# A block's weights and columns ahead of its rows on SyncE's queue, in the routed experts of a graph network

## The chip, the cores and the metric

One core of one Trainium2 chip runs the whole program in one launch. The metric is device time in microseconds (us). Names of the engines: PE is TensorE's matmul (PEld its weight loads), DVE is VectorE, ACT is ScalarE, POOL is GpSimd and SP is SyncE, which does no arithmetic and issues most of the DMAs. Each engine runs its own queue in order, and engines wait for one another and for DMAs by semaphores.

## The reference, cut to what matters

A graph of 3125 nodes with 256 features goes through four pairs of layers, each pair a graph layer and a feed-forward layer with a residual: attention over 53125 edges and a small mixture of experts; a three-layer convolution and a routed mixture of experts; a normalised convolution and a dense mixture of eight experts; a mean convolution and a sliced attention. The change touches the second feed-forward layer alone:

```python
logits = xt @ Wr + br
probs = jax.nn.softmax(logits, axis=-1)
top_p, top_idx = jax.lax.top_k(probs, TOP_K)          # TOP_K = 2 of 8 experts
weights = top_p / top_p.sum(axis=-1, keepdims=True)
xn = (xt - mu) * jax.lax.rsqrt(var + LN_EPS)
xe = xn[None, :, :] * ln_g[:, None, :] + ln_b[:, None, :]
h = jax.nn.gelu(jnp.einsum('end,edh->enh', xe, W1) + b1[:, None, :], approximate=False)
y = jnp.einsum('enh,ehd->end', h, W2) + b2[:, None, :]
y_tok = jnp.transpose(y, (1, 0, 2))
sel = jnp.take_along_axis(y_tok, top_idx[:, :, None], axis=1)
out = (weights[:, :, None] * sel).sum(axis=1)
```

Here D is 256 and the hidden size H is 1024, so an expert's `W1` and `W2` are 1 MB each.

## The kernel before, in words

Where the reference computes every expert for every token, the kernel computes only the two chosen ones. While the last layer of the convolution runs, `Router` takes each group of tokens as it is ready: `normed` normalises it, `gated` makes the gates, `placed` works out each token's place in its expert's list and scatters its row (256 features and 4 numbers: token, two gates, first expert) to `xs_d` in HBM with an indirect DMA of GpSimd (line 997), once for each of its two experts, and `shifted` adds the gated `b2` and stores x to `x_d`. The scatters are collected in `sent`.

`experts1` then pads each expert's list to blocks of 256 rows (BLK) and works out two small tables on VectorE: `block_e`, the expert of each block, and `block_i`, the block's place in `xs_d` (lines 1056 to 1075). SyncE loads these into registers, eight entries at a time (lines 1086 and 1089), because the addresses of its DMAs depend on them. At least 26 blocks (LEAST) run; up to six more would follow behind branches on `block_n`, and in this execution none does.

`block` handles one block:

- its rows `xs` (128 x 2 x 260, 260 KB) come from `xs_d` by a DMA on SyncE's queue (line 1098). `loads_after` makes that DMA wait for all scatters in `sent`. The tile has three buffers;
- its weights and columns come by `Packer.put` (line 181), three DMAs on SyncE's queue into one slot `wslot`: `w1` and `w2`, 1 MB each, and `c`, 13 columns for each partition with the scale and shift of the normalisation, the bias of the first product and the expert's number. The slots rotate through two buffers, so the weights of block i+2 wait until block i has read its own;
- VectorE works out the target rows `to` and the gate from `xs` and `c` (lines 1109 to 1115);
- PE transposes the rows, four 128 x 128 transposes into two PSUM tiles `tr` (line 1120), and VectorE evacuates each with scale and shift into one half of `xe` (line 1122);
- PE makes the hidden layer in eight groups `hid_ps`, each with two products (k = 0 and 1, one for each half of `xe`), into two PSUM buffers; ScalarE empties each with the bias and GELU into `hid` (line 1129). The products are recorded at line 233, in the helper `product`, and each is two records in the profile;
- PE multiplies `hid` by `w2` into `po`, for each of the two halves of the rows; VectorE applies the gate (`ys`, line 1134), and GpSimd adds the rows to `x_d` with an accumulating indirect DMA (line 1135).

The order in the source is not the order on the engines: a scheduler places the instructions on each engine's queue by data that it expects to arrive, while DMAs on SyncE's queue are issued in the order that it gives them. After the last block x is read back from `x_d` and the next convolution starts. `v_rows` (memset at line 2249) is a tile of the later layers that takes over space that the router's tiles had.

Of the kernel before, what the change touches and what calls it, by code (L numbers as in the profile page):

```python
# [22 lines left out]
N, D = 3125, 256  # L23
# [45 lines left out]
def gnn_ffn_kernel(ctx: ExitStack, tc: tile.TileContext, a, out: bass.AP):  # L69
# [157 lines left out]
    def product(ps, terms, bias=None):  # L227

        last = len(terms) - 1
        if bias is not None:  # L230
            nc.tensor.matmul(ps, ones_h[:, :ps.shape[0]], bias, start=True, stop=False)  # L231
        for i, (l, r) in enumerate(terms):
            nc.tensor.matmul(ps, l, r, start=(bias is None and i == 0), stop=(i == last))  # L233
# [110 lines left out]
    def loads_after(loads, sent):  # L344
        for ld in loads:
            for st in sent:
                tc.add_manual_dep(ld.ins, st.ins.name, data_dep, reason="all rows scattered")
# [671 lines left out]
    def experts1(route=None, ahead=lambda: None):  # L1019
# [4 lines left out]
        ec_d = dram.tile([ne, 128, 13], F32, name="ec_d")  # L1024
        with ExitStack() as es:
# [58 lines left out]
            def run(b0, n):  # L1084

                _, at = nc.values_load_multi_w_load_instructions(
                    block_e[0:1, b0:b0 + n], engines=[mybir.EngineType.SP], min_val=0, max_val=ne - 1,
                    skip_runtime_bounds_check_because="a count of 7 comparisons lies in 0..7")
                _, places = nc.values_load_multi_w_load_instructions(
                    block_i[0:1, b0:b0 + n], engines=[mybir.EngineType.SP],  # L1090
                    min_val=0, max_val=8 * EB,
                    skip_runtime_bounds_check_because="a minimum with the last block's place")
                for e, place in zip(at, places):
                    block(e, place)

            def block(e, place):
                xs = pool.tile([128, R, DX], F32, name="xs", bufs=3)
                ld = nc.sync.dma_start(xs, xs_d.rearrange("(b r p) d -> b p r d", p=128, r=R)[
                    ds(place, 1)].rearrange("b p r d -> p (b r) d"))
                loads_after([ld], sent)  # L1100
                wp = Packer()
                w1 = wp.put(a["ex1_W1"][ds(e, 1)].rearrange("e (k p) n -> p (e k) n", p=128), 128,
                            (2, 1024))
                w2 = wp.put(a["ex1_W2"][ds(e, 1)].rearrange("e (k p) n -> p (e k) n", p=128), 128,
                            (8, D))
                c = wp.put(ec_d[ds(e, 1)].rearrange("e p c -> p (e c)"), 128, (13,))
                to = pool.tile([128, R], I32, name="to", bufs=3)
                one, two = (pool.tile([128, R], F32, name=v) for v in ("one", "two"))
                nc.vector.tensor_scalar(one, xs[:, :, R_TOKEN], 0.0, behind, ALU.is_equal, ALU.mult)
                nc.vector.scalar_tensor_tensor(to, xs[:, :, R_TOKEN], -1.0, one, ALU.add, ALU.add)  # L1110
                gate = pool.tile([128, R], F32, name="gate", bufs=3)
                for w, col, op in ((one, R_TOP, ALU.is_equal), (two, R_SECOND, ALU.not_equal)):
                    nc.vector.scalar_tensor_tensor(w, xs[:, :, R_FIRST], c[:, 12:13], xs[:, :, col],
                                                   op, ALU.mult)
                nc.vector.tensor_add(gate, one, two)
                xe = pool.tile([128, 2, BLK], F32, name="xe")
                for k in range(2):
                    ps = psum.tile([128, 512], F32, name="tr")
                    for r in range(R):
                        nc.tensor.transpose(ps[:, r * 128:(r + 1) * 128],  # L1120
                                            xs[:, r, k * 128:(k + 1) * 128], ident)
                    nc.vector.tensor_scalar(xe[:, k, :], ps[:, :BLK], c[:, k:k + 1],  # L1122
                                            c[:, 2 + k:3 + k], ALU.mult, ALU.add)
                hid = pool.tile([128, 8, BLK], F32, name="hid")
                for m in range(8):
                    ps = psum.tile([128, 512], F32, name="hid_ps")
                    product(ps[:, :BLK], [(w1[:, k, m * 128:(m + 1) * 128], xe[:, k, :])
                                          for k in range(2)])
                    nc.scalar.activation(hid[:, m, :], ps[:, :BLK], AF.Gelu, bias=c[:, 4 + m:5 + m])  # L1129
                ys = pool.tile([128, R, D], F32, name="ys")  # L1130
                for r in range(R):
                    po = psum.tile([128, D], F32, name="po")
                    product(po, [(hid[:, m, r * 128:(r + 1) * 128], w2[:, m, :]) for m in range(8)])
                    nc.vector.tensor_scalar(ys[:, r, :], po, gate[:, r:r + 1], None, ALU.mult)
                    nc.gpsimd.indirect_dma_start(
                        out=x_d, in_=ys[:, r, :], in_offset=None, compute_op=ALU.add,
                        out_offset=bass.IndirectOffsetOnAxis(ap=to[:, r:r + 1], axis=0))
# [1185 lines left out]
```

## Time and profile before

| What | Value |
|---|---|
| median of 3 runs | 3920.74 us (3905.55 to 3923.41) |
| the profiled execution | 3903.86 us, its span 3901.7 us |
| PE busy in the span | 3373.3 us (86%) |
| DVE, ACT, POOL busy | 1726.0, 1029.0, 608.9 us |
| mean granted TensorE clock | 0.887 of full speed |
| rows `xs` loaded, first and last issue | 2294.7 and 2647.6 us, 26 times |
| transposes of a block's rows | 104 of 273 ns |
| products `hid_ps` and `po` of the routed blocks | 832 records each, means 387 and 379 ns |
| `hid` on ACT | 208 of 473 ns |

Times within the span are in us from its start. A busy PE is a pipelined one, so its busy time is no measure of how close it is to its peak; what counts for a change is which wait ends last in the stage that it touches. The granted clock is the share of full speed at which TensorE was allowed to run. In a line of the timeline stand the start, the length of the group, the engine, the line of the code, the operation with output and inputs, the number of instructions, and in square brackets the engine's idle time ahead of it with what ended it. In a line of the waits stand the waiting engine and operation, the releaser, and the total, the number and the longest of the waits.

### The profile page before, as it was taken

Reading aid. Unit: us, or ns where it says so; the run is one execution under the profiler, and the core shown is the slowest. Engines: PE = TensorE matmul, PEld = TensorE weight load, DVE = VectorE, ACT = ScalarE, POOL = GpSimd, SP = SyncE. Lnnn points to the kernel's source line nnn. Section 1 sums busy time; section 2 is a strip of 40 time slices with the busy share of each in tenths; the row PEclk is TensorE's granted clock in tenths of the full one; section 3 lists DMA queues with packets and bytes.
Section 4 is the critical chain, followed back from the end, with each engine's and each line's share of the span. In section 5 each row is a group of like instructions: output and inputs, shape, how many; then the busy total and the mean of one; then the engine's idle time right before and its main releaser. Section 6 shows DMA issues by size and latency. Waiting matters only on the chain.

```text
span 3901.7 us, 45135 instructions
## 1 busy us (share of the span) xinstructions
PE 3373.3 (86%) x16645; PEld 2512.7 (64%) x16645; DVE 1726.0 (44%) x4687; ACT 1029.0 (26%) x1931; POOL 608.9 (16%) x588
## 2 busy tenths in 40 slices
PE   6466766766678998999999969997999999999998
PEld 2345545555456566898988858886885555568765
DVE  5345655655676656232335641113562111154562
ACT  1111111111214223333333312222433232242120
POOL 1445445445110000000001222221000000000000
PEclk9677777777768888999999979998989999999998
DMA  5444444444225544434443346665430000023101
GB/s 170 149 143 144 124 138 144 127 134 146 73 66 198 182 162 130 113 99 108 100 105 79 106 126 180 187 170 147 111 86 16 8 17 8 14 69 102 39 1 34
DMA packets 265707, 415.30 MB, mean 106 GB/s; under 512 B 40860, under 2 KB 206273, under 8 KB 265473
## 3 DMA queue, kind: packets, MB, share of 16 engines
q1 hardware_dynamic: 200242, 261.56, 22.9%
q0 software_dynamic: 51568, 134.33, 12.5%
q10 hardware_dynamic: 13663, 16.39, 1.6%
q8 instruction: 135, 2.21, 0.2%
q14 instruction: 99, 0.81, 0.1%
HBM read 313.72 MB, written 98.40 MB: 106 GB/s over the span
## 4 chain that ended last, share of the span: by engine, by line
PE 61%; DVE 2%; DMA 1%; ACT 1%; issue 0%; POOL 0%; SPq 0%; ACTq 0%; DVEq 0%; POOLq 0%
PE po L233 19%; PE agg L2057 18%; PE hid_ps L233 13%; PE tr L233 2%; PE row L233 1%; PE tok L1436 1%; PE po L231 1%; PE tr L223 1%; DMA x_d<-ys,to 1%; PE tr L2131 1%; PE bk L1966 1%; PE bk L1954 0%; ACT h L1277 0%; PE bdeg L1956 0%; PE pair L233 0%
## 5 line engine op out<-in xcount | busy, mean ns | idle before, releaser
L2057 PE MATMUL agg<-cnt_f,hp 125*128 125x500 f32 (+1 forms) x3500 | 734.4, 370 | 24.0 <-ACT hp L1998 24.0
L2057 PEld LDWEIGHTS agg<-cnt_f,hp 125*128 125x128 f32 x3500 | 638.7, 190 | 108.4 <-ACT hp L1998 25.3
L1556 POOL DMA_INDIRECT kv<-kv_d,src_w x450 | 437.4, 972 | 468.5 <-PE acc L1777 323.9
L2035 ACT CAST cnt_f<-blk 125x500 fp32r<-125x500 bf16 (+1 forms) x435 | 245.9, 566 | 479.4 <-PE agg L2057 464.1
L1732 PE MATMUL qx<-q_t,oht 125*128 125x256 bf16 x1350 | 260.2, 357 | 128.8 <-issue 76.8
L2035 DVE CAST cnt_f<-blk 125x500 fp32r<-125x500 bf16 (+1 forms) x440 | 185.2, 422 | 293.3 <-PE agg L2057 249.5
L1732 PEld LDWEIGHTS <-oht 125*128 125x128 bf16 x1350 | 165.5, 125 | 200.6 <-issue 150.5
L1283 DVE SCALAR_TENSOR_TENSOR x<-po,gall,x 125x256 f32<-125x256 f32 x200 | 93.8, 484 | 416.2 <-PE po L233 415.7
L1277 ACT ACTIVATE h<-hid_ps,shift,scale 128x500 f32<-128x500 f32 (+1 forms) x224 | 161.7, 722 | 376.0 <-PE hid_ps L233 375.5
L1777 PE MATMUL acc<-kv,oh_f 128*125 128x265 f32 x900 | 211.6, 395 | 20.3 <-DVE kv L1770 20.3
L1735 DVE TENSOR_TENSOR kv<-kv,qx 128x512 f32<-128x512 f32 x225 | 147.0, 681 | 146.2 <-remote 122.0
L1777 PEld LDWEIGHTS acc<-kv,oh_f 128*125 128x125 f32 x900 | 169.8, 191 | 59.3 <-DVE kv L1770 28.0
L233 PE MATMUL hid_ps<-xe,wslot 128*128 128x256 f32 x832 | 194.8, 387 | 11.3 <-DVE xe L1122 11.2
L233 PE MATMUL po<-wslot,h 128*125 128x256 f32 x800 | 203.0, 386 | 0.1
L233 PE MATMUL hid_ps<-h,wslot 128*128 128x500 f32 (+1 forms) x448 | 192.5, 552 | 4.1 <-ACT h L1277 0.6
L233 PEld LDWEIGHTS po<-wslot,h 128*125 128x125 f32 x800 | 145.0, 187 | 75.2 <-ACT h L1277 27.2
L233 PE MATMUL hid_ps<-v_rows,wslot 128*128 128x500 f32 (+1 forms) x448 | 187.2, 538 | 0.0
L233 PE MATMUL po<-wslot,hid 128*128 128x256 f32 x832 | 183.8, 379 | 0.0
L233 PEld LDWEIGHTS hid_ps<-xe,wslot 128*128 128x128 f32 x832 | 148.8, 191 | 44.7 <-DVE xe L1122 14.4
L997 POOL DMA_INDIRECT xs_d<-r_l,pos x50 | 59.5, 1190 | 723.0 <-DVE r_l L993 598.9
L233 PEld LDWEIGHTS po<-wslot,hid 128*128 128x128 f32 x832 | 158.1, 190 | 21.5
L1129 ACT ACTIVATE hid<-hid_ps,wslot 128x256 f32<-128x256 f32 x208 | 96.8, 473 | 279.9 <-PE hid_ps L233 279.9
(480 smaller groups left out, 4683.2 us busy)
## 6 DMA issues: line engine op xcount, KB each, us to landing
wslot<-in_ex_W SPq DMA_DIRECT2D x52, 1024.0 KB
blk<-an_d SPq DMA_DIRECT2D x60, 546.9 KB
xs_d<-nothing SPq DMA_DIRECT2D x10, 2730.0 KB
blk<-at_d SPq DMA_DIRECT2D x40, 546.9 KB
blk<-an_d SPq DMA_DIRECT2D x45, 410.2 KB
at_d<-ab SPq DMA_DIRECT2D x25, 683.6 KB
an_d<-an SPq DMA_DIRECT2D x25, 683.6 KB
blk<-at_d SPq DMA_DIRECT2D x30, 410.2 KB
```

Of the source, the lines that this page charges most:

```text
L223: nc.tensor.transpose(ps[:, i * P:(i + 1) * P], src[:, i, k * 128:(k + 1) * 128], ident[:P, :P])
L233: nc.tensor.matmul(ps, l, r, start=(bias is None and i == 0), stop=(i == last))
L997: st = nc.gpsimd.indirect_dma_start(out=xs_d, in_=l2[:, i, :], in_offset=None, out_offset=bass.IndirectOffsetOnAxis(ap=self.pos[s][:, t0 + ...
L1129: nc.scalar.activation(hid[:, m, :], ps[:, :BLK], AF.Gelu, bias=c[:, 4 + m:5 + m])
L1277: nc.scalar.activation(dst[:, m, :c], ps[:, :c], AF.Relu, bias=shift[:, l, col:col + 1], scale=scale[:, l, col:col + 1])
L1283: nc.vector.scalar_tensor_tensor(x[:, t0 + i, :], po, gating.all[:, t0 + i, e:e + 1], x[:, t0 + i, :], ALU.mult, ALU.add)
L1556: nc.gpsimd.indirect_dma_start(out=kv[:, c, KO:], out_offset=None, in_=kv_d, in_offset=bass.IndirectOffsetOnAxis(ap=src_i[:, at + c:at + c ...
L1732: nc.tensor.matmul(ps[:, c, :], s.oht[:, p * PC + c0 + c, :], s.q[:, k, :], start=(k == 0), stop=(k == 2))
L1735: nc.vector.tensor_mul(k_, k_, ps)
L1777: nc.tensor.matmul(s.acc[:, :D + H + 1], of[:, c, :], kv[:, c, AO:VO], start=(p == 0 and c == 0), stop=(p == 2 and c == PC - 1))
L2035: to(f[:, :n, :], part[0][:, :n, m % MB, :])
L2057: nc.tensor.matmul(ps[f][:, :c], hp[:, m, k, f * 128:(f + 1) * 128], got[:, :c], start=(m == 0 and k == 0), stop=(m == T - 1 and k == 1))
```

## The change

In `block` the three DMAs of the packer move ahead of the DMA of the rows, and among them the columns `c` move ahead of the two weights. On SyncE's queue a block's DMAs stood as rows, W1, W2, columns; they now stand as columns, W1, W2, rows. Nothing is added or removed, and the dependencies are the same: only the rows wait for the scatters.

```diff
             def block(e, place):
+                wp = Packer()
+                c = wp.put(ec_d[ds(e, 1)].rearrange("e p c -> p (e c)"), 128, (13,))
+                w1 = wp.put(a["ex1_W1"][ds(e, 1)].rearrange("e (k p) n -> p (e k) n", p=128), 128,
+                            (2, 1024))
+
+                w2 = wp.put(a["ex1_W2"][ds(e, 1)].rearrange("e (k p) n -> p (e k) n", p=128), 128,
+                            (8, D))
                 xs = pool.tile([128, R, DX], F32, name="xs", bufs=3)
                 ld = nc.sync.dma_start(xs, xs_d.rearrange("(b r p) d -> b p r d", p=128, r=R)[
                     ds(place, 1)].rearrange("b p r d -> p (b r) d"))
                 loads_after([ld], sent)
-                wp = Packer()
-                w1 = wp.put(a["ex1_W1"][ds(e, 1)].rearrange("e (k p) n -> p (e k) n", p=128), 128,
-                            (2, 1024))
-                w2 = wp.put(a["ex1_W2"][ds(e, 1)].rearrange("e (k p) n -> p (e k) n", p=128), 128,
-                            (8, D))
-                c = wp.put(ec_d[ds(e, 1)].rearrange("e p c -> p (e c)"), 128, (13,))
```

## The prediction

> **What bounds the kernel now.** I read the page first, for the weight of each engine, then the change's stage alone: the timeline and the windows around the routed blocks.
>
> ```profile
> span 3901.7 us, 45135 instructions
> ...
> PE 3373.3 (86%) x16645; PEld 2512.7 (64%) x16645; DVE 1726.0 (44%) x4687; ACT 1029.0 (26%) x1931; POOL 608.9 (16%) x588
> ```
>
> PE is the engine to follow, and the stage is PE's more than the rest: the 26 blocks run from 2294.7 us (first rows issued) to 2689.8 us (last matmul: 2682.77 + 7.07), and from 2322.33 to 2689.80 the windows give PE 363.73 us busy of 367.47, at a granted clock of 1.00. So no transfer holds the steady blocks; only a change in PE's own order or in what PE waits for can move them. The waits of this stretch say the same. Each line is who waited for whom: us in total, times, longest.
>
> ```profile
> DVE one L1113 <- DMA wslot<-ec_d: 189.8, 23, 9.2
> ...
> PE hid_ps L233 <- DVE xe L1122: 3.6, 6, 0.6
> ...
> PEld hid_ps L233 <- ACT hid L1129: 4.9, 24, 0.6
> ```
>
> The first is the largest wait that the change removes: VectorE stands 8.3 us in each block for the columns `c`, which land behind 2 MB of weights. But PE is hardly behind it: it waited 3.6 us for `xe`, in six blocks.
>
> Those six are what the forecast rests on. The order of the built programs shows why. In before, the transposes of the next block are spread through PE's queue among the matmuls of the present one, in a cycle of four blocks. Every fourth block (starting at 2365.50, 2424.28, 2483.07, 2541.85, 2600.63, 2659.42) has all four transposes of its own directly ahead of its first product. PE's timeline of a block without transposes and of the one after it (start, us, group, idle before):
>
> ```profile
> 2351.67 7.09 PE L233 MATMUL hid_ps<-xe,wslot 128*128 128x256 f32 x32
> 2358.59 7.07 PE L233 MATMUL po<-wslot,hid 128*128 128x256 f32 x32
> ...
> 2365.50 0.60 PE L1120 MATMUL tr<-ident,xs 128*128 128x128 f32 x4
> 2366.69 1.99 PE L233 MATMUL hid_ps<-xe,wslot 128*128 128x256 f32 x8 [0.59 <-DVE xe L1122]
> 2368.52 0.38 PE L1120 MATMUL tr<-ident,xs 128*128 128x128 f32 x2
> 2368.87 5.45 PE L233 MATMUL hid_ps<-xe,wslot 128*128 128x256 f32 x24
> 2374.15 7.07 PE L233 MATMUL po<-wslot,hid 128*128 128x256 f32 x32
> 2381.06 0.38 PE L1120 MATMUL tr<-ident,xs 128*128 128x128 f32 x2
> ```
>
> The block without transposes takes 13.83 us (2351.67 to 2365.50), the next one 15.56 (2365.50 to 2381.06), the two others of a cycle 14.70 each: 58.79 for four, 14.70 on average.
>
> **Steady blocks in the changed program.** Its order on PE is the same for every block: four transposes, 16 products into `hid_ps`, 16 into `po`; nothing of the next block lies between. The scheduler now sees rows that arrive after the weights and puts the transposes last. So every block has the shape of the 15.56 us block. Its parts: 1.19 us from the transposes to the first product (0.60 of transposes, 0.59 idle until VectorE has `xe`), and then a second hole. The first four products stand as m0 k0, m1 k0, m0 k1, m1 k1 in both programs' blocks of this shape, so the first GELU starts late (2368.34, 0.47 us long, so done at 2368.81), and the third group, which needs its PSUM buffer, starts at 2368.87. In before, two transposes of the next block fill this hole (0.38 us). In the changed program nothing does, but the start at 2368.87 is set by ScalarE, not by them, so taking them out should give nothing back. Bounds: at best the hole goes with them, and the block takes 13.82 + 1.19 = 15.01; at worst it stays, 15.56. I take 15.56: the weight load of the third group waited 0.20 us for ScalarE even after the two transposes.
>
> The sum: blocks 1 to 25 run from 2322.33 to 2689.84 = 367.51 us. Changed: 24 x 15.56 + 15.72 for the last (2365.50 to the end of its `po`, 2374.15 + 7.07) = 389.16. That is **+21.65 us**. With 15.01 it is about +7.9.
>
> **Do the rows still come in time?** The rows of block i+2 now stand behind the columns and both weights of block i+2, and these wait for the slot that block i's last `po` frees. In before SyncE issues block i+3's rows right after block i+2's columns, a whole block earlier. From the freed slot (first weight issue) to the columns, the last of the 2 MB, it took 9.06 us (2351.83 to 2360.89), in others 8.7 to 10.1 (2498.93 to 2508.99). The rows add 260 KB: at 2.1 MB in 9.1 us, 1.2 us more, so they land 10 to 11.4 us after the slot is free. Their transposes come one block later, 15.56 us. Over 4 us of cover, so I cost the lost block of lead at nothing; if that cover went, each us of lateness would cost 25 us. VectorE now waits for rows instead of columns, ahead of `ys` of the present block; `ys` is ready some 12 us into it, so it is late by a fraction of a us, with two `po` buffers behind it.
>
> **The first block.** The change's promise lies here: weights that need not wait for the rows' scatters. But the block's expert number does not come earlier.
>
> ```profile
> 2287.12 1.19 POOL L997 DMA_INDIRECT xs_d<-r_l,pos  x1 [0.30 <-issue]
> 2291.40 0.18 DVE L1070 TENSOR_TENSOR be<-be,ge 1x32 f32<-1x32 f32 x1 [6.10 <-DMA xs_d<-r_l,pos]
> 2291.42 0.08 DVE L2249 MEMSET v_rows<- 128x25 f32 x1
> ...
> 2292.95 0.16 DVE L1073 CAST block_e<-be 1x32 int32<-1x32 f32 x1
> ...
> 2294.74 0.43 SPq L1098 DMA_DIRECT2D xs<-xs_d  x1
> ```
>
> VectorE stands 6.10 us for the last scatter, because a memset of `v_rows` (into freed space that the scatters still read) is queued among the operations that make `block_e`; it is there in the changed program too. `block_e` is cast 0.31 us before `block_i`, and that is all the weights gain. The same bytes (rows, two weights, columns) then stand ahead of the first product, but the rows are last: in before the last of them let VectorE go at 2305.53, after the four transposes were long done at 2298.8. Now those (1.09 us, at a clock of 0.50), the small VectorE work and the first `xe` (0.54 us) follow the landing: first product 0.4 to 1.0 us later than 2306.39. Block 0 loses the two transposes that it carries for block 1 (0.2 to 0.4). I take **+0.5**, bounds -0.5 and +2 (the clock stays at 0.52 from 2306.39 to 2310.20, and where it rises may shift). Nothing after the stage is overlapped with it: PE's next work waits for x to be read back.
>
> **Clock.** The granted clock was 1.00 in the 15.56 us block in spite of its hole of 0.59 us, so I price the new holes at their length alone. The Trainium skill, "TensorE: Matmul & The Clock Gate", section "A second HAM failure mode: psum-queue depth-cycling", speaks against this: frequent short idles between groups of matmuls can make the clock fall and rise. With that page's window of about 3.4 us at half rate in each of 25 blocks, an estimate is 1.7 x 25 = some 43 us more.
>
> **Total.** 21.65 + 0.5 = +22.15. The profiled execution took 3903.86 (2.2 around its span), so it would become 3926.0. The three runs have their median at 3920.74, 17 us above; on it the forecast is **3942.9**. What a measurement of this kernel can tell from no change is about 0.5%, 19.6 us; the forecast is just beyond it.
>
> **The rivals.**
> 1. The second hole closes without the two transposes: 15.01 per block, +7.9 + 0.5 = +8.4, 3929.1. For it: nothing of the next block is left on PE. Against: ScalarE's time above.
> 2. Rows late: if contention with the weights and with the scatters to `x_d` pushes rows from 11.4 to 16 us after the slot is free, each block waits 0.5 us or more: +12.5 on top, about 3955. The cover of 4 us speaks against it.
> 3. Not slower: the first block's weights do run ahead of the scatters, and the steady blocks keep 14.70. It decides where `block_e` reaches SyncE before the last scatter has landed (2287.12 + 3.84 = 2290.96). VectorE had 2 us of work left after its stand (2291.40 to 2293.43), so `block_e` could be there near 2287, the weights issued 1.3 us later (as 2293.43 to 2294.74) and landed 9.1 us after that, the rows 1.2 us behind them at 2298.6, and the first product some 1.5 us on, near 2300.1, 6.3 us earlier: 3920.74 - 6.3 = 3914.4. Against it: the memset's place, and PE's order, which alone costs over three times that. To be faster by over 0.5% all blocks would have to come near 13.83, with transposes that cost nothing.
>
> **How the numbers follow.** Forecast 0.66, of which 0.14 is taken as falling just under 19.6 us; rival 1 0.12; rival 2 or the clock 0.14; rival 3 0.08, of which 0.05 beyond the bound through what I have not seen. Slower: 0.52 + 0.14 = 0.66. Same: 0.14 + 0.12 + 0.03 = 0.29. Faster 0.05. Range: low end rival 1 on the lowest run, 3905.55 + 8.4 = 3914; high end the forecast with rival 2 on the highest, 3923.41 + 22.15 + 12.5 = 3958. The forecast alone spans 3927.7 to 3945.6 over those runs.
>
> **What would show it.** Right: 25 starts of four transposes 15.5 us apart; PE waiting for `xe` some 0.6 us in each of 25 blocks (15 us instead of 3.6) and its weight loads for ScalarE; VectorE's long wait put down to `xs` instead of `ec_d`; `block_e` still at about 2293. Wrong: PE waiting for `xs` in steady blocks, a period near 15.0 or 14.7, a granted clock under 1.00 there, or a first product well before 2306.

## The result, and the profile after

The changed kernel takes 3941.81 us (median; 3936.1 to 3946.88) against 3920.31 us (3905.55 to 3923.41) before: a ratio of 1.0058, 95% interval 1.0041 to 1.0074, or +21.5 us (+16 to +29). The forecast was +22.15 us and 3942.9 us.

The page of the changed kernel, its first lines:

```profile
span 3945.0 us, 45106 instructions
...
PE 3391.3 (86%) x16645; PEld 2518.3 (64%) x16645; DVE 1730.0 (44%) x4687; ACT 1029.4 (26%) x1931; POOL 609.5 (15%) x588
```

PE runs as many instructions as before and is busy 18 us longer. The two spans differ by 43.3 us, twice what the runs show, so the difference has to be cut up first. The stage is measured here, and in every experiment, from the matmul that adds up the tokens' counts (line 1050, just ahead of `block_e`) to the issue that reads x back after the last block. Ahead of the stage the profiled execution lost 15.87 us (2296.34 against 2280.47), behind it 6.02 (1211.31 against 1205.29), and in it 21.41 (437.35 against 415.94). Only the stage holds changed code, and its 21.41 us agree with the 21.5 by which the medians differ. The rest is taken as the difference between two executions: the runs of before alone lie 18 us apart.

The waits of the steady blocks (2322 to 2712 us; engine and operation, releaser, total us, times, longest):

```profile
DVE one L1110 <- DMA xs<-xs_d: 208.6, 24, 9.9
...
PEld hid_ps L233 <- DVE xe L1123: 19.9, 24, 0.8
PE hid_ps L233 <- DVE xe L1123: 14.2, 24, 0.6
PEld hid_ps L233 <- ACT hid L1130: 14.0, 24, 0.6
PE hid_ps L233 <- ACT hid L1130: 4.2, 23, 0.2
```

VectorE's long wait has changed its name from `ec_d` (189.8 us, longest 9.2) to `xs` (208.6, longest 9.9). PE's wait for `xe` has gone from six blocks to each of the 24 in the window, and a wait that before had once (0.2 us) now comes in nearly every block: the third group of products waits for ScalarE. There is no PE wait for a DMA. PE's timeline of one block:

```profile
2368.47 0.60 PE L1121 MATMUL tr<-ident,xs 128*128 128x128 f32 x4
2369.66 1.99 PE L233 MATMUL hid_ps<-xe,wslot 128*128 128x256 f32 x8 [0.59 <-DVE xe L1123]
2371.83 5.45 PE L233 MATMUL hid_ps<-xe,wslot 128*128 128x256 f32 x24 [0.18 <-ACT hid L1130]
2377.12 7.10 PE L233 MATMUL po<-wslot,hid 128*128 128x256 f32 x32
2384.05 0.60 PE L1121 MATMUL tr<-ident,xs 128*128 128x128 f32 x4
```

It has the shape of the longest of the four blocks in before's cycle, 15.58 us (2368.47 to 2384.05), and every block has it: the transposes of blocks 1 to 25 start from 2337.35 to 2711.37, 24 steps of 15.58 us. The windows give the whole stretch of blocks 1 to 25 at full clock (us, then busy PE, PEld, DVE, ACT, POOL with their instructions, clock, DMA share, GB/s):

```profile
2337.35:2727.12 389.77, 370.45 (x1701) 306.43 (x1699) 66.07 (x220) 92.44 (x200) 77.55 (x50) 1.00 0.57 164
```

389.77 us against 367.51 (2322.33 to 2689.84 in before), so +22.26. The first block went the other way. Its timeline:

```profile
2307.29 0.18 DVE L1070 TENSOR_TENSOR be<-be,ge 1x32 f32<-1x32 f32 x1 [6.12 <-DMA xs_d<-r_l,pos]
...
2308.85 0.16 DVE L1073 CAST block_e<-be 1x32 int32<-1x32 f32 x1
...
2310.07 0.39 SPq L181 DMA_DIRECT2D wslot<-ec_d  x1
2310.67 0.96 SPq L181 DMA_DIRECT2D wslot<-in_ex_W  x2
...
2312.75 0.37 SPq L1105 DMA_DIRECT2D xs<-xs_d  x1
...
2319.56 0.23 DVE L1110 TENSOR_SCALAR one<-xs,behind 128x2 f32<-128x2 f32 x1 [10.23 <-DMA xs<-xs_d]
...
2319.67 1.09 PE L1121 MATMUL tr<-ident,xs 128*128 128x128 f32 x4 [22.75 <-DMA xs<-xs_d]
...
2320.97 7.24 PE L233 MATMUL hid_ps<-xe,wslot 128*128 128x256 f32 x21 [0.21 <-DVE xe L1123]
```

and, for the same place in before, the lines that the prediction did not show:

```profile
2295.98 0.96 SPq L181 DMA_DIRECT2D wslot<-in_ex_W  x2
...
2305.53 0.22 DVE L1113 SCALAR_TENSOR_TENSOR one<-xs,wslot 128x2 f32<-128x2 f32 x1 [7.51 <-DMA wslot<-ec_d]
...
2306.39 3.78 PE L233 MATMUL hid_ps<-xe,wslot 128*128 128x256 f32 x8 [7.60 <-DVE xe L1122]
```

From the end of the stand for the scatters (2307.29, before 2291.40) to the first product it took 13.68 us against 14.99, and to block 1 30.06 against 30.93: -0.87 us (-0.85 from the start of the stage).

### The profile page after: what moved, and what is told of

It is laid out like the page before. It is cut to its first block, busy times and chain, and to the rows that moved or that the text cites. A ratio compares the mean times of both kernels' runs of the same rounds, so it can differ in the third digit from the quotient of the medians.

```text
span 3945.0 us, 45106 instructions
## 1 busy us (share of the span) xinstructions
PE 3391.3 (86%) x16645; PEld 2518.3 (64%) x16645; DVE 1730.0 (44%) x4687; ACT 1029.4 (26%) x1931; POOL 609.5 (15%) x588
## 3 DMA queue, kind: packets, MB, share of 16 engines
q0 software_dynamic: 51568, 134.33, 12.5%
## 4 chain that ended last, share of the span: by engine, by line
PE 61%; DVE 3%; DMA 2%; ACT 1%; issue 1%; POOL 0%; SPq 0%; ACTq 0%; DVEq 0%; POOLq 0%
PE po L233 19%; PE agg L2058 18%; PE hid_ps L233 13%; PE tr L233 2%; PE row L233 1%; PE tok L1437 1%; PE po L231 1%; PE tr L223 1%; DMA x_d<-ys,to 1%; PE tr L2132 1%; PE bk L1967 1%; PE bk L1955 0%; ACT h L1278 0%; PE bdeg L1957 0%; PE s L233 0%
```

## The experiments

The theory on trial is the prediction's: the time goes into PE's order (all four transposes of a block directly ahead of its own products, with two holes behind them), the transfers themselves cost nothing, and the order comes from the place of the rows. Against it stand the rivals that it is the transfers (rows or weights that land late, or compete), or another part of the change. What each expected of a run is quoted with the run.

Four runs (the columns alone, the rows alone, the change with three buffers, the change with the memset moved) share a chip on which before takes 3609.36 us; the other four share one on which it takes 3916.17 us. The 300 us lie ahead of the stage: its first matmul starts at 1978 to 1981 us on the one, at 2284 to 2290 on the other, and at 2280 and 2296 in the two profiles above. So lengths of the stage are compared across both chips, and times only as ratios. A length of the stage comes from one profiled execution of each kernel, and block 0 in it varies by up to 1.4 us with the moment at which the clock rises (last section); the steady blocks do not. Period is the mean distance of steady blocks.

| kernel | ratio of times, 95% interval | stage, us | against 415.94 |
|---|---|---|---|
| the change | 1.0058 (1.0041 to 1.0074) | 437.35 | +21.41 |
| columns ahead of the weights, rows first as before | 1.0000 (0.9991 to 1.0009) | 413.44 | -2.50 |
| rows behind the weights and columns | 1.0056 (1.0041 to 1.0072) | 434.74 | +18.80 |
| the change, three PSUM buffers `hid_ps` | 1.0028 (1.0018 to 1.0039) | 426.02 | +10.08 |
| before, three PSUM buffers `hid_ps` | 1.0029 (1.0017 to 1.0041) | 426.06 | +10.12 |
| the change, memset of `v_rows` on GpSimd | 1.0058 (1.0044 to 1.0071) | 431.81 | +15.87 |
| before, products pipelined in the source | 0.9977 (0.9966 to 0.9987) | 404.92 | -11.02 |
| the change, products pipelined in the source | 1.0035 (1.0020 to 1.0049) | 429.75 | +13.81 |
| the parts that paid, together | 0.9947 (0.9931 to 0.9964) | 399.35 | -16.59 |

### Which half of the change: the columns alone, the rows alone

Columns alone, against before:

```diff
 ld = nc.sync.dma_start(xs, ...)
 loads_after([ld], sent)
 wp = Packer()
+c = wp.put(ec_d[...], 128, (13,))
 w1 = wp.put(a["ex1_W1"][...], 128, (2, 1024))
 w2 = wp.put(a["ex1_W2"][...], 128, (8, D))
-c = wp.put(ec_d[...], 128, (13,))
```

> Only the columns move: rows, columns, W1, W2. Theory A (the cost sits in PE's order, which follows the place of the rows): the cycle of four blocks stays, 58.8 us for four, so no loss in the steady blocks; the first product needs the columns and W1 instead of the columns behind W2, so it starts up to 5 us after W1 instead of after everything: 0 to -6 us against before. Theory B (the columns' place makes the scheduler or VectorE late): blocks of 15.59 us, some +20 us against before.

Measured: no difference in time, 1.0000 (0.9991 to 1.0009). PE's four-block cycle is kept in the build and in the profile: PE waits for `xe` in 7 blocks, not in all. PE's timeline of block 0 and the start of block 1:

```profile
2002.11 9.39 PE L233 MATMUL hid_ps<-xe,wslot 128*128 128x256 f32 x32 [3.32 <-DMA wslot<-in_ex_W]
2011.34 7.10 PE L233 MATMUL po<-wslot,hid 128*128 128x256 f32 x32
2018.28 0.60 PE L1120 MATMUL tr<-ident,xs 128*128 128x128 f32 x4
2019.47 1.99 PE L233 MATMUL hid_ps<-xe,wslot 128*128 128x256 f32 x8 [0.59 <-DVE xe L1122]
```

With the columns early, `xe` is ready before W1, and the first product needs W1 alone, not all 2 MB: it starts 21.55 us after the count's matmul against 25.92. Of these 4.4 us, 1.9 are given back by a longer block 0 and because the cycle now starts with a long block (block 1 stands above, in the 15.56 us shape): the stage is 2.50 us shorter, which the time is too coarse to show.

Rows alone, against before (on SyncE's queue W1, W2, columns, rows):

```diff
-xs = pool.tile([128, R, DX], F32, name="xs", bufs=3)
-ld = nc.sync.dma_start(xs, ...)
-loads_after([ld], sent)
 wp = Packer()
 w1 = wp.put(a["ex1_W1"][...], 128, (2, 1024))
 w2 = wp.put(a["ex1_W2"][...], 128, (8, D))
 c = wp.put(ec_d[...], 128, (13,))
+xs = pool.tile([128, R, DX], F32, name="xs", bufs=3)
+ld = nc.sync.dma_start(xs, ...)
+loads_after([ld], sent)
```

> Only the rows move: W1, W2, columns, rows. Theory A (PE's order follows the place of the rows): the same shape in every block as with the whole change, 15.59 us each, +20 to +23 us against before. Theory B (the columns make it): the cycle of four stays and the time is that of before, within 4 us.

Measured: 1.0056 (1.0041 to 1.0072), about the whole loss of the change (18.80 us in the stage, a little under the 20 expected), with a period of 15.56 us. Its waits in the steady blocks:

```profile
PE hid_ps L233 <- DVE xe L1122: 14.8, 25, 0.6
PEld hid_ps L233 <- ACT hid L1129: 14.0, 24, 0.6
...
PE hid_ps L233 <- ACT hid L1129: 4.2, 23, 0.2
```

They are those of the changed kernel. So the rows' new place is what costs. Of the 2.6 us that the change's stage is longer, 1.9 lie ahead of block 1, 1.3 of them in block 0 itself; blocks 1 to 25 differ by 0.7 us, so in them the columns' new place is worth 0.03 us each.

### Transfers or PE's order: a third PSUM buffer, with each order of the DMAs

If the second hole is the wait for a PSUM buffer that ScalarE has to empty, one buffer more closes it, and the other products and transfers stay as they are. Against the change, and the same line against before:

```diff
-ps = psum.tile([128, 512], F32, name="hid_ps")
+ps = psum.tile([128, 512], F32, name="hid_ps", bufs=3)
```

> The whole change with three PSUM buffers for hid_ps instead of two. Theory A (two holes per block: 0.59 us for xe, and about 0.4 us until the first GELU frees a PSUM buffer): the second hole closes, the first stays; 15.1 to 15.2 us a block, 10 to 12 us less than the changed kernel, +9 to +12 against before; PE's wait for ScalarE goes. Rival (the period is set by the rows' arrival or by the slot): still 15.59 us, +21.

> The DMA order of before (rows first, columns last) with three PSUM buffers for hid_ps; in this build PE's order has the four transposes of each block directly ahead of its own products, as in the change. Theory A (the loss is PE's order; where rows and columns stand on SyncE's queue costs nothing once PE's order is given): the same 15.13 us a block as the change with three buffers, so +9 to +12 us against before. Rival (the DMA order itself costs): rows are a block early here, so blocks of 14.7 us or less and the time of before or better.

Measured: 1.0028 (1.0018 to 1.0039) and 1.0029 (1.0017 to 1.0041). PE's timeline of the change with three buffers:

```profile
2064.50 0.60 PE L1121 MATMUL tr<-ident,xs 128*128 128x128 f32 x4
2065.70 7.17 PE L233 MATMUL hid_ps<-xe,wslot 128*128 128x256 f32 x32 [0.59 <-DVE xe L1123]
2072.71 7.09 PE L233 MATMUL po<-wslot,hid 128*128 128x256 f32 x32
2079.64 0.60 PE L1121 MATMUL tr<-ident,xs 128*128 128x128 f32 x4
```

and of before with three buffers:

```profile
2376.56 0.60 PE L1120 MATMUL tr<-ident,xs 128*128 128x128 f32 x4
2377.75 7.17 PE L233 MATMUL hid_ps<-xe,wslot 128*128 128x256 f32 x32 [0.59 <-DVE xe L1122]
2384.76 7.07 PE L233 MATMUL po<-wslot,hid 128*128 128x256 f32 x32
2391.67 0.60 PE L1120 MATMUL tr<-ident,xs 128*128 128x128 f32 x4
```

The 32 products run through in one line; the hole between the first eight records and the others is gone, and the block takes 15.13 us on average instead of 15.58. PE's only wait left is the one for `xe`, 14.8 us in 25 blocks. From block 1 to the end of the stage before takes 374.08 us, the change 396.34 and the change with three buffers 385.05. So of the change's 21.41 us the second hole is 11.29, the transposes that stand alone ahead of `xe` are 10.97, and the first block is -0.85.

The pair tells more than either run. With three buffers the scheduler gives before the uniform order too, four transposes, 16 products, 16 products. Now both kernels have the same order on PE and differ only in the order of DMAs: in the one the rows come a block early and the columns last, in the other the reverse. Their periods are 15.13 and 15.11 us, and from block 1 on they take 385.05 and 384.61 us; that the whole stages agree to 0.04 us (426.02 and 426.06) is luck, for block 0 differs by as much the other way. So in steady blocks the transfers' order by itself costs at most 0.02 us each, 0.4 in all; what it does, it does through the order that PE's queue is built in. Before, with its DMAs where they were, loses 10.12 us of the stage once it has this order. The pair also shows that late rows are not the only thing that brings the uniform order about: a hole in the scheduler's plan that asks to be filled seems to be needed as well, and the third buffer takes it away. That is read from the built orders; the scheduler's reasons were not tested.

### The stand for the scatters: the memset on another engine

Against the change, the memset that keeps `block_e` behind the last scatter goes to GpSimd:

```diff
-nc.vector.memset(v[:, :, D:], 1.0)
+nc.gpsimd.memset(v[:, :, D:], 1.0)
```

> The whole change with the memset of v_rows on GpSimd, behind its scatters, instead of VectorE, where block_e stands behind it. Theory A (block_e is held by that memset alone): SyncE issues the first weights about 1.3 us after a block_e that comes some 6 us earlier, they land while the scatters run, and the first product starts 4 to 7 us earlier; the steady blocks keep 15.59 us; +14 to +18 against before. Rival (the weights' slot or the transfers hold the first block): no gain, +21.

Measured: 1.0058 (1.0044 to 1.0071); the time alone does not tell it from the change. The profile does:

```profile
1986.77 0.23 DVE L1073 CAST block_e<-be 1x32 int32<-1x32 f32 x1
...
1988.69 0.39 SPq L181 DMA_DIRECT2D wslot<-ec_d  x1
1989.29 0.96 SPq L181 DMA_DIRECT2D wslot<-in_ex_W  x2
1991.19 0.14 POOL L2250 MEMSET v_rows<- 128x25 f32 x1 [3.21 <-DMA xs_d<-r_l,pos]
1991.38 0.37 SPq L1105 DMA_DIRECT2D xs<-xs_d  x1
```

`block_e` stands 6.6 us after the count's matmul (1980.1) instead of 12.5, and columns and weights are issued ahead of the landing of the last scatter, for which only GpSimd's memset and the rows' DMA still wait. The first product comes 4.2 us earlier than in the change (20.43 against 24.63 after the count), and the stage is 5.54 us shorter; from block 1 to the end it is the change's to the hundredth (396.34 us in both). The other 1.34 us are a shorter block 0, in which the clock rose earlier; that is no part of the mechanism. The gain rests on this one profile: by the medians the run is 20.9 us slower than before, not the 14 to 18 expected. This is rival 3's mechanism, with the memset that held it named rightly: against before the first product comes 5.5 us earlier, where the prediction put 6.3.

### What the change would do to another order on PE

In these two kernels the source is pipelined: `block` is split into loads with transposes (`block`), the hidden products (`hidden`) and the output products (`output`), and the next block's rows are transposed between the hidden and the output products of the present one.

```diff
+                for e, place in run(b0, min(8, LEAST - b0)):
+                    following = block(e, place)
+                    if got is not None:
+                        output(got, hid)
+                    got = following
+                    hid = hidden(got)
+            output(got, hid)
...
-                run(b0, min(8, LEAST - b0))
```

> The DMA order of before with the same source order; the built order has the four transposes between the hidden layer and the output. Theory A: no hole is left, only the transposes' own 0.43 to 0.5 us: 13.82 + 0.5 = 14.3 us a block against 14.70, 8 to 11 us less than before. Rival (xe or GELU still shows): 14.7 us, no gain.

> The change's DMA order, with the source written so that a block's loads, transposes and xe stand between the hidden layer and the output of the block before; the built order has the four transposes after six of the sixteen output products. Theory A: both holes go; but the rows are wanted 9.5 us after the slot is free (6.91 + 6 x 0.43) and land 10 to 11 us after it, so PE waits for them 0.5 to 1.4 us in each block: 14.8 to 15.7 us a block, +2 to +24 us against before, put down to xs. Rival (rows are never late): 14.3 us a block, 10 to 12 us less than before.

Measured: with before's order of DMAs 0.9977 (0.9966 to 0.9987), with the change's 1.0035 (1.0020 to 1.0049). PE's timeline of the first:

```profile
2371.37 7.09 PE L233 MATMUL hid_ps<-xe,wslot 128*128 128x256 f32 x32
2378.30 0.60 PE L1124 MATMUL tr<-ident,xs 128*128 128x128 f32 x4
2378.73 7.07 PE L233 MATMUL po<-wslot,hid 128*128 128x256 f32 x32
2385.64 7.09 PE L233 MATMUL hid_ps<-xe,wslot 128*128 128x256 f32 x32
```

PE's waits in the steady blocks are gone, for `xe` and for ScalarE, and the period is 14.27 us, below before's mean of 14.70: the evacuation to `xe` now lies beside 16 output products, and both halves are there before the block begins. The second, with the rows behind the weights (here the scheduler put the transposes after six of the 16 output products):

```profile
2378.96 2.76 PE L233 MATMUL po<-wslot,hid 128*128 128x256 f32 x12
...
2382.32 0.63 PE L1124 MATMUL tr<-ident,xs 128*128 128x128 f32 x4 [0.61 <-DMA xs<-xs_d]
...
2382.79 4.50 PE L233 MATMUL po<-wslot,hid 128*128 128x256 f32 x20
2387.13 7.09 PE L233 MATMUL hid_ps<-xe,wslot 128*128 128x256 f32 x32
```

Its PE has two waits in the steady blocks:

```profile
PE tr L1124 <- DMA xs<-xs_d: 18.2, 23, 1.8
PE tr L1124 <- SPq L1164: 1.8, 1, 1.8
```

Here PE does wait for rows, in each of 24 blocks, 20.0 us in all (18.2 put down to the DMA itself, 1.8 to SyncE), and the steps between blocks are 15.0 to 16.3 us, 15.33 on average. So the order of the DMAs that costs next to nothing when PE takes the transposes last costs 24.83 us (429.75 - 404.92) when it takes them early, 20.0 of them in this wait (the place of the transposes among the output products differs between the two as well): rival 2, late rows, is real in this kernel and absent in the changed one.

### Together

This kernel pipelines the source, keeps rows, columns, W1, W2 for the steady blocks, uses columns, W1, W2, rows for block 0 alone (`first`), and has the memset on GpSimd:

```diff
-            def block(e, place):
+            def block(e, place, first=False):
...
+                if not first:
+                    xs = rows()
 wp = Packer()
 ...
+                if first:
+                    xs = rows()
```

> Pipelined source order; for the first block alone columns, W1, W2, rows; for all others rows, columns, W1, W2; memset of v_rows on GpSimd. Theory A: 14.3 us a block (-9 us) and a first product 4 to 6 us earlier: 13 to 16 us less than before (ratio 0.9957 to 0.9964). Rival (the first block is bound by 2.4 MB of transfers whatever the order): only the 9 us.

Measured: 3896.80 us against 3916.17, 0.9947 (0.9931 to 0.9964), so half a per cent under before, and somewhat more than the 13 to 16 us expected (16.59 in the stage). Its period is 14.29 us, and its first product comes 20.42 us after the count, as in the run with the memset moved.

## Why the prediction was right, and where one term was wrong

**PE's order, right.** Every block took the 15.56 us shape (15.58 measured), 389.16 us predicted for blocks 1 to 25 and 389.77 measured. The first hole is 0.59 us as read from before's long block.

**The second hole, right.** The choice between 15.01 and 15.56 went to ScalarE and the PSUM buffer, and the third buffer shows that this is the wait. Rival 1, a hole that closes with the two transposes, is out. Its 15.01 was a little low: with the hole closed by a buffer the block takes 15.13.

**The rows, right, for a reason that does not carry far.** In the steady blocks they were in use on VectorE 9.9 to 11.2 us after the columns' issue (2369.09 to 2379.18 and 2384.35 to 2394.40 are two), about the 10 to 11.4 predicted and ahead of the 15.58 at which PE asks for them. (The 9.06 us of the prediction starts at 2351.83, which in the chain of work is the start of a row of products; the weights' issue stands at 2351.97, which makes it 8.92 and leaves the cover as it was.) But the cover was there because PE's order had moved the transposes to the end. The pipelined pair shows what the same lateness costs without it, 0.83 us of PE's wait in each block.

**The clock, right.** It was granted at 1.00 from 2337.35 to 2727.12 with two holes in every 15.58 us. The fall that the Trainium skill's page "TensorE: Matmul & The Clock Gate" describes under "A second HAM failure mode: psum-queue depth-cycling", an estimated 43 us, did not occur with these holes of 0.59 and 0.18 us; at what holes it would was not tried.

**The first block, wrong in size and sign.** Predicted +0.5 (bounds -0.5 to +2), measured -0.87. The first product, forecast 0.4 to 1.0 us later, came 1.31 us earlier after the stand (13.68 against 14.99). The term that failed is "`block_e` is cast 0.31 us before `block_i`, and that is all the weights gain". `block_e` itself came no earlier (1.56 us after the stand, before 1.55), as predicted. But the weights' issue came 1.20 us earlier (3.38 us after the stand, before 4.58): in before they stood on SyncE's queue behind the rows' issue, and 1.24 us lie between the two issues (2294.74 to 2295.98), while behind the columns it is 0.60 (2310.07 to 2310.67); the other 0.56 is the first issue itself, 2.78 us after the stand instead of 3.34. From the weights' issue to the last landing that VectorE waits for it took 8.89 us against 9.55 to that point, 0.66 less; why was not tried. The tail behind the last landing grew by 0.55 (1.41 us from VectorE's start to the first product, before 0.86), as the prediction had reasoned. Block 0 itself, where 0.2 to 0.4 less was expected, took 0.44 more (16.38 against 15.94), because the clock rose later. The windows of 1 us in which it rose, before's first and then the change's:

```profile
2309.40:2310.40 1.00, 1.00 (x5) 0.71 (x5) 0.00 (x0) 0.19 (x1) 0.00 (x0) 0.67 1.12 321
...
2325.00:2326.00 1.00, 1.00 (x4) 0.82 (x3) 0.05 (x1) 0.26 (x1) 0.00 (x0) 0.53 0.14 43
```

Read as a step from 0.50 to 1.00 (a mean of 0.67 is a third of the window at 1.00), they put the rise 5.0 us after the first product in the change and 3.7 in before, and at half speed that is worth 0.65 us. The four parts: -1.20 - 0.66 + 0.55 + 0.44 = -0.87.

**The cause of the order, half right.** "The scheduler now sees rows that arrive after the weights and puts the transposes last" holds so far as moving the rows is enough (rows alone) and moving the columns is not (columns alone). It is not the only way: before with three buffers has the same order with its rows a block early.

**The sum, right, and in part by luck; the profiled execution, no guide to it.** +22.15 predicted, 21.41 in the stage and +21.5 (+16 to +29) in the times. Two misses partly cancel: the steady blocks took 0.61 us more than forecast, the first block 1.35 less. Set against the profiled execution, the forecast of 3926.0 misses 3946.88 by 21 us, as much as the two profiles differ outside the stage (21.89).

## What to carry to other kernels

A DMA's place in a queue can cost nothing as a transfer and still cost time through a scheduler that places instructions by expected arrival: compare the built order of the busiest engine before asking whether data will be late, and price the changed order by a block of the old profile that already has that shape. Short work that another engine must finish before PE can go on belongs among long work that does not depend on it: the transposes of the next block between the hidden and the output products of the present one were worth 11.02 us of the stage against before's mixed order. Where an order of loads helps the first block and hurts the steady ones, give it to the first block alone.

## What was not expected of the hardware

The clock's rise does not follow the first product at a fixed distance. PE starts block 0 at a granted clock of 0.50 in each of five kernels, and windows of 1 to 2 us put the rise at 2.2 us after the first product with the memset moved, 2.2 in the kernel with all parts together, 3.7 in before, 4.6 with the columns alone and 5.0 in the change. At half speed this spread of 2.8 us is worth 1.4, about the 1.34 us between block 0 taking 15.04 us with the memset moved (2000.57 to 2015.61) and its 16.38 in the change. What sets the rise was not tried.

Two chips ran the same program 300 us apart, and nearly all of it in the first quarter of the execution: in the attention over the edges the products of line 1732 had a median of 404 ns and ended at 1023 us in the execution of before that is shown here, and 272 ns and 727 us on the other chip (columns alone, whose code there is the same). The granted clock in the first 500 us was 0.76 and 0.92 (0.76 too in before with three buffers, on the chip of the 3916 us). The routed blocks ran alike on both.
